# Two graph layers on one core: node preparation in four pieces, early masks and node tables on GpSimd, the first two rounds written out

## The chip, the core and the metric

The kernel runs on one NeuronCore of a Trainium2 chip. Five engines work beside each other, each through its own instructions in order: TensorE (PE) multiplies matrices, VectorE (DVE) and ScalarE (ACT) work element by element, GpSimd (POOL) does the same with general processors and also issues transfers, and SyncE (SP) issues most transfers. Engines wait for each other with semaphores. SBUF is the working memory of 128 partitions; PSUM is where PE writes its results, and POOL can't reach it.

The metric is the device time of one execution in microseconds (us). Smaller is better.

## The reference

There are N = 3327 nodes with D = 64 features and a 0/1 matrix `adj` (N by N). Two layers follow each other; each normalizes its input, takes the positive part `h`, and adds its result to `x`.

```python
# layer 0, on h = relu(layernorm(x))
x_t = logmap0(x, c)
left, right = x_t @ w_att[:D, 0], x_t @ w_att[D:, 0]
adj_att = sigmoid(left[:, None] + right[None, :] + b_att[0]) * adj
x_local = logmap(x[:, None, :], x[None, :, :], c)         # every pair of nodes
support_t = einsum('ij,ijd->id', adj_att, x_local)
return proj(expmap(x, support_t, c), c)
# layer 1, on h = relu(layernorm(x))
mask = (adj != 0); rank = cumsum(mask, axis=1); deg = rank[:, -1:]
k = minimum(deg, 100); pos = rank - (deg - k)
w = mask * where(pos > 0, 0.5 ** (k - pos), 0.0)          # the last neighbours of a row weigh most
return w @ (h @ weight) + bias
```

Layer 0 needs, for every pair of nodes, a sigmoid, the product of the two nodes' features and a function of it. Layer 1 needs, for every place of `adj`, the number of neighbours behind it in its row.

## The kernel before, in words

The nodes are padded to 26 blocks of 128. The function `fast` does all the work (`general` is a branch for inputs outside a range; it isn't entered here). The rows of the result are cut into four strips of 8, 8, 6 and 4 blocks. In each strip, a round takes one column block of `adj`, from the last to the first (two in the strip of 4), so that a round holds 128 x 1024 elements or 128 x 768. There are 91 rounds. One round does this, each step a function of its own:

- `load` (L613 to L618) brings the round's piece of the transposed `adj` into a tile `ad`, 512 KB, issued by SP; five tiles are in use in turn.
- `edges` (L620 to L623) makes the mask `ad != 0` in bf16, on DVE.
- `count` (L625 to L636) adds it, on PE, to a running number of neighbours in PSUM (`pc`), with two triangular constant matrices `ca` and `cb`.
- `read` (L638 to L649) takes the positive part out of `pc` into a small integer tile kept for layer 1. In strip 0 every second one is ACT's (`ON_ACT`), the others are DVE's.
- `sigmoids` (L651 to L656): ACT, a tanh of `left` (spread along the strip, `left_b`) with `right` as the bias.
- `products` (L668 to L674): PE, four matmuls into a tile `pq` in PSUM, of which there are two, from the features as columns (`ju`, `jz`) and as rows (`iu`, `iz`).
- two Gelu activations on `pq` in place (ACT, L1211 and L1212, in strip 0's first round L879 and L880).
- `pair_one` (L661) and `pair_two` (L666): DVE, sigmoid plus one times `ad`, and then times the function in `pq`.
- `total` (L676 to L684): PE, the sum over the round with the node table `hw` (65 columns, float32) into `po`.

After a strip, `post` finishes its nodes, with many small instructions on POOL, and after the last strip a second stage does layer 1's product (L1255 on).

Order: a manual schedule keeps PE, DVE and ACT in the order in which the code asks for work. POOL's and SP's instructions are placed by a scheduler, so the order of their lines in the code isn't the order in which they run. The loop at L1194 works n rounds at a time in a pipeline: while it multiplies round n, it makes the mask of n + 2, counts and reads n + 1, and prepares the sigmoids and products of n + 1.

Before the loop stands the preparation, which the change is about:

- x comes in two halves of 13 blocks, one issued by SP and one by ACT (L455, L456). For each half DVE takes the mean (L715) and the difference (L716), and ACT three activations (L717 to L719); then DVE reduces four times (L721, L722).
- A chain of small DVE instructions of 26 to 52 elements follows (L749 to L781 and L811 to L825): a Newton iteration for the inverse roots and constants of each node. Each mostly needs the one before it.
- `features` (L784) scales the features of the blocks that are needed first (strip 0's own blocks 0 to 7 and column blocks 24, 25); PE turns them (L831 to L838); copies bring them to `iu`, `ju`, `iz`, `jz` (L839 to L842). POOL's transfers (L846) copy them once more into `ju` and `jz` for the rounds that use blocks 0 to 7 as columns.
- The same follows for the column blocks 16 to 23 (`high`) and later 8 to 15 (`low`): `features`, casts, `turned_to` (L792), `kept` (L796, L797), and `logits` (L862 to L866) for `left` and `right`.
- Round 0 and the beginning of round 1 are written out between these (L869 to L899). The loop starts with round 1; in its first three passes it does `last_of_ahead`: the turning of `low`, the table `hw` in two parts (L907 to L915), the row of `left` sent to DRAM and back (L596 to L598), and eleven small constants of the nodes (L917 to L927).

Of the kernel before, what the change touches and what calls it, by code (L numbers as in the profile page):

```python
# [11 lines left out]
F32 = mybir.dt.float32  # L12
# [10 lines left out]
P = 128  # L23
N = 3327
NB = 26
# [7 lines left out]
AHEAD, LOADS = 1, 4  # L33
SGB, ADB = 5, 5
# [411 lines left out]
def fast(ctx, tc, x, adj_t, r, w_att, b_att, weight, bias, out, flag):  # L446
# [8 lines left out]
    nc.sync.dma_start(x_sb[:, :13], xv[:, :13])  # L455
    nc.scalar.dma_start(x_sb[:, 13:], xv[:, 13:])  # L456
# [137 lines left out]
    def left_to_dram():  # L594
        plt = ps.tile([P, P], F32, name="po")
        T.transpose(plt[:NB, :], left, ident)  # L596
        V.tensor_copy(left_t, plt[:NB, :])
        nc.sync.dma_start(left_d.rearrange("(b p) -> b p", p=P), left_t)  # L598
# [21 lines left out]
    def edges(n):  # L620
        mask_of[n] = mask = work.tile([P, FMAX], BF16, name="mask", bufs=3)
        args = mask[:, : span(n)], ad_of[n][:, : span(n)]
        V.tensor_scalar(*args, 0.0, None, op0=ALU.not_equal)  # L623
# [14 lines left out]
    def read(n, j):  # L638
        k, lo, hi = rounds[n]
        S = strips[k]  # L640
        kept = behind(j)[:, S.i0 : S.i0 + S.F]
        num, den = ON_ACT[k]
        i = NB - 1 - j
        if i * num // den != (i + 1) * num // den:
            A.activation(kept, S.pc[:, : S.F], AF.Relu, scale=128.0 if j in JD else 1.0)  # L645
        elif j in JD:
            V.tensor_scalar(kept, S.pc[:, : S.F], 0.0, 128.0, op0=ALU.max, op1=ALU.mult)
        else:
            V.tensor_scalar(kept, S.pc[:, : S.F], 0.0, None, op0=ALU.max)  # L649
# [63 lines left out]
    for hs in node_halves:  # L713
        n = hs.stop - hs.start
        V.tensor_reduce(m[:, hs], x_sb[:, hs], AX.X, ALU.add)  # L715
        V.scalar_tensor_tensor(d[:, hs], wide(m[:, hs], n), -1.0 / D, x_sb[:, hs], op0=ALU.mult, op1=ALU.add)  # L716
        A.activation(sq[:, hs], d[:, hs], AF.Square)  # L717
        A.activation(rl[:, hs], d[:, hs], AF.Relu)
        A.activation(sr[:, hs], rl[:, hs], AF.Square)  # L719
# [47 lines left out]
    G.memset(ju[D : KB + 7, first_i], -WB * QS)  # L767

# [29 lines left out]

    A.activation(g, g2, AF.Ln, bias=one_c, scale=-0.5)
# [26 lines left out]
    edges(0)  # L826
# [20 lines left out]

    V.tensor_mul(yr, yr, g[:, :NB])
# [6 lines left out]
    def logits(bs):  # L855

        plr = ps.tile([P, NB, 2], F32, name="po")
# [10 lines left out]
    for j in js(0):  # L868
        count(0, j)  # L869
    logits((first_i, last_j))  # L870
    V.tensor_sub(nz[:, high, 1], zf[:, high], nz[:, high, 0])
    for j in js(0):
        read(0, j)
# [3 lines left out]
    edges(1)  # L877
    pq = pq_of[0]
    A.activation(pq, pq, AF.Gelu, scale=-WG / QS)  # L879
    A.activation(pq, pq, AF.Gelu, scale=WH)  # L880
# [4 lines left out]
    for j in js(1):  # L885
        count(1, j)
    products(1)
    edges(2)
# [3 lines left out]
    for j in js(1):  # L892
        read(1, j)
    pair_two(0)
    logits((high,))
    features(low)
    A.copy(nz[:, low, 0], zf[:, low])
    V.tensor_copy(nu[:, low, :D], zf[:, low])
    V.tensor_sub(nz[:, low, 1], zf[:, low], nz[:, low, 0])  # L899

    def last_of_ahead():

        p4 = ps.tile([P, 16, P], F16, name="po")
        turned_to(p4, low, 0)
        kept(p4, low, 0)
        wn, opx = small("wn"), small("opx")
        V.tensor_scalar(wn, nrm, WA / 2, None, op0=ALU.mult)  # L907
        V.tensor_scalar(opx, x2, c_c, 1.0, op0=ALU.mult, op1=ALU.add)
        V.tensor_mul(hw[:, :, D], opx, wn)
        V.tensor_mul(wn, wn, y)  # L910
        V.tensor_mul(hw[:, 13:, :D], rl[:, 13:], wide(wn[:, 13:], 13))
        logits((low,))
        left_to_dram()
        yield
        V.tensor_mul(hw[:, :13, :D], rl[:, :13], wide(wn[:, :13], 13))  # L915
        yield
        V.tensor_scalar(w2s, w2, 2.0**27 / HS, None, op0=ALU.mult)  # L917
        V.tensor_scalar(ih, babs, 2 / WA, None, op0=ALU.mult)
        V.tensor_scalar(balm, bal, MIN_NORM, None, op0=ALU.max)
        V.tensor_mul(su, nrm, balm)  # L920
        V.tensor_mul(sv, bal, su)
        V.reciprocal(sk, balm)
        V.tensor_scalar(sk, sk, sqc, None, op0=ALU.mult)
        V.tensor_scalar(maxnorm, absr, 1.0 - EPS_BALL, None, op0=ALU.mult)
        V.tensor_mul(c2_c, c_c, c_c)
        V.tensor_scalar(m2c, c_c, -2.0, None, op0=ALU.mult)
        V.tensor_scalar(p2c, c_c, 2.0, None, op0=ALU.mult)  # L927
        ahead.close()

        behind_of["lo"] = ctx.enter_context(tc.tile_pool(name="lo", bufs=1, side="right", reuse_waits="tile")).tile(  # L930
            [P, JD.start, NP], U8, name="behind_lo")
        yield
# [261 lines left out]
    for n in range(1, R):  # L1194
# [7 lines left out]
        two = m < R and len(js(m)) == 2  # L1202
# [7 lines left out]
        pq = pq_of[n][:, :w]  # L1210
        A.activation(pq, pq, AF.Gelu, scale=-WG / QS)  # L1211
        A.activation(pq, pq, AF.Gelu, scale=WH)  # L1212
# [5 lines left out]
        if m + 1 < R:  # L1218
            edges(m + 1)
        if two:  # L1220
            read(m, js(m)[0])
        if m < R:
            count(m, js(m)[-1])
        if n + 1 < R:
            sigmoids(n + 1)
        if m < R:
            read(m, js(m)[-1])
        if n + 1 < R:
            products(n + 1)
        if n > 1 and not turned and not early:  # L1230
            total(n - 2)
# [148 lines left out]
```

## Time and profile before

| | |
|---|---|
| median of three executions | 418.3 us (418.13, 418.3, 419.4) |
| profiled execution, whole time | 419.95 us |
| its span in the profile | 418.2 us |
| mean granted TensorE clock | 0.973 |
| busy: PE, DVE, ACT, POOL | 359.9, 377.5, 362.8, 113.4 us |
| bytes moved | 48.99 MB, mean 117 GB/s |
| largest groups on DVE | L666 103.5 us, L661 103.8 us, L623 58.7 us |
| largest group on PE | L683 162.2 us |

The profile is one execution. Its span runs from the first to the last instruction that it saw; the whole time is somewhat longer. An engine's busy time is the time in which it executed; issuing transfers and waiting for semaphores are not in it. A row of a view in order of time gives the start, the duration, the engine with the line, the operation, the tile written and the tiles read, the shapes, and in brackets the engine's idle time before the instruction and what ended it. Instructions on DVE and ACT overlap a little, so that the time from one start to the next can be some 0.08 us less than the duration.

### The profile page before, as it was taken

The numbers are of one execution on the slowest core, as the hardware profiler recorded it, in microseconds if no ns is written. First come the engines' busy times: TensorE is split into PE (matmuls) and PEld (weight loads), VectorE is DVE, ScalarE is ACT, GpSimd is POOL, SyncE is SP. The second block draws the span as 40 slices with busy tenths as digits, with TensorE's granted clock in tenths as the row PEclk, the third lists the DMA queues.
The fourth block names the chain that finished last, engine by engine and source line by source line (L and its number), as shares of the span: only waits on it lengthen the run. The fifth ranks groups of instructions, "written<-read, shape, count | busy, mean of one in ns | idle before, by whom it ended". The sixth has DMA issues, their size and how long they took to land. (4 is left out here: it accounts for less than half of the span.)

```text
span 418.2 us, 4717 instructions
## 1 busy us (share of the span) xinstructions
PE 359.9 (86%) x1460; PEld 154.2 (37%) x1460; DVE 377.5 (90%) x559; ACT 362.8 (87%) x409; POOL 113.4 (27%) x224
## 2 busy tenths in 40 slices
PE   0094999999998899999999899999877999898792
PEld 0062333333333333333333444444332333344362
DVE  4989999999999999999999998899989899898841
ACT  3577889999999999999999999999896999787810
POOL 7020000000000073950250063801405183442400
PEclk9999799999999999999999999999898999999987
DMA  7313634444547445444535455444633420000012
GB/s 180 160 40 102 191 100 153 150 153 150 155 146 233 138 127 175 141 121 143 147 116 159 113 152 146 123 146 127 186 116 103 113 88 0 2 0 1 2 25 65
DMA packets 23298, 48.99 MB, mean 117 GB/s; under 512 B 8789, under 2 KB 9245, under 8 KB 23265
## 3 DMA queue, kind: packets, MB, share of 16 engines
q1 hardware_dynamic: 20993, 47.66, 37.9%
q0 software_dynamic: 464, 0.49, 0.7%
q10 hardware_dynamic: 1808, 0.46, 0.6%
q8 instruction: 13, 0.21, 0.2%
q14 instruction: 20, 0.16, 0.1%
HBM read 46.40 MB, written 0.87 MB: 113 GB/s over the span
## 5 line engine op out<-in xcount | busy, mean ns | idle before, releaser
L683 PE MATMUL po<-sg,hw 128*65 128x512 f32 (+1 forms) x364 | 162.2, 570 | 0.4 <-DVE st L958 0.4
L666 DVE SCALAR_TENSOR_TENSOR sg<-pq,sg 128x1024 f32<-128x1024 f32 (+1 forms) x91 | 103.5, 1137 | 7.4 <-ACT pq L1212 6.8
L661 DVE SCALAR_TENSOR_TENSOR sg<-sg,ad 128x1024 f32<-128x1024 f32 (+1 forms) x91 | 103.8, 1140 | 0.1
L656 ACT ACTIVATE sg<-left_b,right 128x1024 f32<-128x1024 f32 (+2 forms) x103 | 99.5, 978 | 0.0
L1211 ACT ACTIVATE pq<-pq 128x1024 f32<-128x1024 f32 (+1 forms) x90 | 86.1, 957 | 2.7 <-PE pq L674 2.5
L1212 ACT ACTIVATE pq<-pq 128x1024 f32<-128x1024 f32 (+1 forms) x90 | 85.2, 946 | 2.9
L683 PEld LDWEIGHTS po<-sg,hw 128*65 128x65 f32 x364 | 49.7, 139 | 70.8 <-issue 56.9
L634 PE MATMUL pc<-mask,ca 128*128 128x512 bf16 (+1 forms) x175 | 64.3, 368 | 12.4 <-DVE behind_hi L649 3.8
L673 PE MATMUL pq<-iu,ju 71*128 71x512 f16 (+1 forms) x182 | 67.8, 373 | 1.5 <-ACT jz L797 1.0
L635 PE MATMUL pc<-mask,cb 128*128 128x512 bf16 (+1 forms) x182 | 65.5, 370 | 1.8 <-ACT behind_lo L645 1.7
L674 PE MATMUL pq<-iz,jz 128*128 128x512 f16 (+1 forms) x182 | 66.3, 371 | 0.0
L623 DVE TENSOR_SCALAR mask<-ad 128x1024 bf16<-128x1024 f32 (+1 forms) x91 | 58.7, 645 | 0.0
L1280 PE MATMUL pw<-wt,s 128*128 128x512 bf16 (+1 forms) x154 | 34.2, 376 | 4.2 <-DVE s L1135 2.2
L635 PEld LDWEIGHTS <-cb 128*128 128x128 bf16 x182 | 17.9, 98 | 53.2 <-issue 41.5
L1030 POOL TENSOR_TENSOR dots<-dots,ih 128x8 f32<-128x8 f32 (+1 forms) x3 | 2.2, 720 | 129.0 <-DVE dots L1050 129.0
L634 PEld LDWEIGHTS <-ca 128*128 128x128 bf16 x175 | 17.3, 99 | 29.6 <-issue 17.7
L1280 PEld LDWEIGHTS <-s 128*128 128x128 f16 x182 | 18.0, 101 | 23.8 <-issue 4.3
L673 PEld LDWEIGHTS <-ju 71*128 71x128 f16 x182 | 18.0, 99 | 22.8 <-DVE sg L666 4.3
L674 PEld LDWEIGHTS <-jz 128*128 128x128 f16 x182 | 18.1, 100 | 19.5 <-issue 2.3
L645 ACT ACTIVATE behind_lo<-pc 128x1024 uint8<-128x1024 f32 (+2 forms) x29 | 24.9, 858 | 0.0
L645 ACT ACTIVATE behind_hi<-pc 128x1024 uint8<-128x1024 f32 (+2 forms) x23 | 19.7, 858 | 5.6 <-PE pc L635 5.6
L1285 POOL TENSOR_TENSOR x_sb<-x_sb,bias_b 128x256 f32<-128x256 f32 (+1 forms) x6 | 9.9, 1657 | 51.0 <-DVE w L1119 45.5
(317 smaller groups left out, 366.8 us busy)
## 6 DMA issues: line engine op xcount, KB each, us to landing
ad<-in_adj_t SPq DMA_DIRECT2D x65, 512.0 KB, 3.6
ad<-in_adj_t SPq DMA_DIRECT2D x26, 384.0 KB, 3.2
out<-o SPq DMA_DIRECT2D x6, 128.0 KB, 1.9
left_b<-left_d SPq DMA_DIRECT2D x1, 512.0 KB, 4.0
x_sb<-in_x ACTq DMA_DIRECT2D x1, 416.0 KB, 5.6
x_sb<-in_x SPq DMA_DIRECT2D x1, 416.0 KB
left_b<-left_d SPq DMA_DIRECT2D x1, 384.0 KB
jz<-iz POOLq DMA_DIRECT2D x2, 128.0 KB, 2.6
```

The source lines that it names most:

```text
L623: V.tensor_scalar(*args, 0.0, None, op0=ALU.not_equal)
L634: T.matmul(S.pc[:, f0:f1], ca, S.before[:, f0:f1], start=False, stop=True, skip_group_check=True)
L635: T.matmul(S.pc[:, f0:f1], cb, now[:, f0:f1], start=S.first, stop=True, skip_group_check=True)
L656: A.activation(part(n, sg, j), S.left[:, : S.F], AF.Tanh, bias=right[:, j : j + 1], scale=0.5)
L661: V.scalar_tensor_tensor(sg, sg, 1.0, ad_of.pop(n)[:, :w], op0=ALU.add, op1=ALU.mult)
L666: V.scalar_tensor_tensor(sg, pq_of.pop(n)[:, :w], WD, sg, op0=ALU.add, op1=ALU.mult)
L673: T.matmul(part(n, pq, j, f0, f1), ju[:KB, j, :], S.iu[:, f0:f1], start=True, stop=False)
L674: T.matmul(part(n, pq, j, f0, f1), jz[:, j, :], S.iz[:, f0:f1], start=False, stop=True)
L683: T.matmul(S.po[: D + 1, f0:f1], hw[:, j, :], part(n, sg_of[n], j, f0, f1), start=j == NB - 1, stop=j == 0)
L1211: A.activation(pq, pq, AF.Gelu, scale=-WG / QS)
L1212: A.activation(pq, pq, AF.Gelu, scale=WH)
L1280: T.matmul(pw[n], s2[:, j].rearrange("p c d -> p (c d)"), wt[:, f0:f1].bitcast(BF16), start=j == order[0], stop=j == NB - 1)
```

## The change

- x comes in four pieces of 7, 6, 7 and 6 blocks, issued by SP and ACT in turn, and the first loop on it runs over these pieces. The four reductions stay on halves.
- `edges` takes an engine. The masks of rounds 0 to 2 (`EARLY`) are made on POOL, which compares with zero twice (`is_equal`, `is_equal`); those of later rounds stay on DVE.
- `read` takes an order to use ACT. Rounds 0 to 2 use it. `count` and `read` of round 0 move to the place before the logarithms of the preparation.
- The table `hw` is made on POOL, in seven pieces of up to 4 blocks, the last blocks first. Nine of the eleven node constants move to POOL; `balm` and its reciprocal stay on DVE.
- The features of `low` are made between rounds 0 and 1, turned into a `pq` tile (not `po`), and the logits of `low` and the row of `left` use the same tile.
- Rounds 0 and 1 are written out whole; the loop starts with round 2, and two pieces of `adj` more than four are loaded ahead of it.

In the program as built, POOL runs after its first constants the masks of rounds 0, 1 and 2, then five small constants, then `opx`, `ih`, `wn`, the seven pieces of `hw`, and only then the transfers of the turned features. On PE `count` of round 0 stands ahead of the transposes, and `count` of round 1 right behind them, ahead of the first logits.

```diff
+EARLY = 3
...
-    nc.sync.dma_start(x_sb[:, :13], xv[:, :13])
-    nc.scalar.dma_start(x_sb[:, 13:], xv[:, 13:])
+    pieces = (slice(0, 7), slice(7, 13), slice(13, 20), slice(20, NB))
+    for n, part in enumerate(pieces):
+        (nc.scalar if n % 2 else nc.sync).dma_start(x_sb[:, part], xv[:, part])
...
-    def edges(n):
+    def edges(n, E=V):
         mask_of[n] = mask = work.tile([P, FMAX], BF16, name="mask", bufs=3)
         args = mask[:, : span(n)], ad_of[n][:, : span(n)]
-        V.tensor_scalar(*args, 0.0, None, op0=ALU.not_equal)
+        if E is G:
+            G.tensor_scalar(*args, 0.0, 0.0, op0=ALU.is_equal, op1=ALU.is_equal)
+        else:
+            V.tensor_scalar(*args, 0.0, None, op0=ALU.not_equal)
...
-    def read(n, j):
+    def read(n, j, on_act=None):
...
-        if i * num // den != (i + 1) * num // den:
+        if on_act or (on_act is None and i * num // den != (i + 1) * num // den):
...
-    for hs in node_halves:
+    for hs in pieces:
...
     G.memset(ju[D : KB + 7, first_i], -WB * QS)
+    for n in range(EARLY):
+        edges(n, G)
...
+    for j in js(0):
+        count(0, j)
+        read(0, j, True)
     A.activation(g, g2, AF.Ln, bias=one_c, scale=-0.5)
...
-    edges(0)
...
+    wn, opx = small("wn"), small("opx")
+    G.tensor_scalar(wn, nrm, WA / 2, None, op0=ALU.mult)
+    G.tensor_scalar(opx, x2, c_c, 1.0, op0=ALU.mult, op1=ALU.add)
+    G.tensor_mul(hw[:, :, D], opx, wn)
+    G.tensor_mul(wn, wn, y)
+    for b in (24, 20, 16, 12, 8, 4, 0):
+        n = min(4, NB - b)
+        G.tensor_mul(hw[:, b : b + n, :D], rl[:, b : b + n], wide(wn[:, b : b + n], n))
...
-    for j in js(0):
-        count(0, j)
+    for j in js(1):
+        count(1, j)
     logits((first_i, last_j))
     V.tensor_sub(nz[:, high, 1], zf[:, high], nz[:, high, 0])
-    for j in js(0):
-        read(0, j)
+    for j in js(1):
+        read(1, j, True)
     products(0)
     pl = first_left()
     turned_to(p3, high, 0)
-    edges(1)
...
+    gelus(0)
     strips[0].left, left_b = pl, strips[0].left
     sigmoids(0)
     kept(p3, high, 0)
     pair_one(0)
-    for j in js(1):
-        count(1, j)
+    features(low)
+    V.tensor_copy(nu[:, low, :D], zf[:, low])
     products(1)
-    edges(2)
...
     sigmoids(1)
-    for j in js(1):
-        read(1, j)
+    A.copy(nz[:, low, 0], zf[:, low])
     pair_two(0)
     logits((high,))
...
+    for j in js(2):
+        count(2, j)
+    pair_one(1)
     V.tensor_sub(nz[:, low, 1], zf[:, low], nz[:, low, 0])
+    gelus(1)
+    p5 = ps.tile([P, FMAX], F32, name="pq", bufs=2)
+    p4 = p5.bitcast(F16).rearrange("p (b q) -> p b q", q=P)
+    turned_to(p4, low, 0)
+    total(0)
+    sigmoids(2)
+    edges(3)
+    kept(p4, low, 0)
+    for j in js(2):
+        read(2, j, True)
+    pair_two(1)
+    products(2)
+    logits((low,), p5[:, : 2 * NB].rearrange("p (b c) -> p b c", c=2))
+    left_to_dram(p5[:, FMAX - P :])
...
     def last_of_ahead():
-        p4 = ps.tile([P, 16, P], F16, name="po")
-        turned_to(p4, low, 0)
-        kept(p4, low, 0)
...
-        V.tensor_mul(hw[:, 13:, :D], rl[:, 13:], wide(wn[:, 13:], 13))
-        logits((low,))
-        left_to_dram()
+        V.tensor_scalar(balm, bal, MIN_NORM, None, op0=ALU.max)
+        V.reciprocal(sk, balm)
         yield
-        V.tensor_mul(hw[:, :13, :D], rl[:, :13], wide(wn[:, :13], 13))
-        yield
-        V.tensor_scalar(w2s, w2, 2.0**27 / HS, None, op0=ALU.mult)
+        G.tensor_scalar(w2s, w2, 2.0**27 / HS, None, op0=ALU.mult)
...
     load(LOADS)
-    for n in range(1, R):
+    load(LOADS + 1)
+    for n in range(2, R):
```

## The prediction

> **What bounds the kernel now.** I read the table of busy times, then the busy times in stretches, then DVE's and POOL's rows in order of time up to 60 us, and last the few rows where POOL and DVE work side by side.
>
> ```profile
> span 418.2 us, 4717 instructions
> PE 359.9 (86%) x1460; PEld 154.2 (37%) x1460; DVE 377.5 (90%) x559; ACT 362.8 (87%) x409; POOL 113.4 (27%) x224
> ...
> 34.00:44.00 10.00, 4.44 (x44) 2.66 (x44) 9.28 (x19) 7.59 (x10) 0.00 (x0) 0.82 0.37 116
> 44.00:54.00 10.00, 10.00 (x29) 3.61 (x28) 9.37 (x20) 8.04 (x8) 0.19 (x1) 0.84 0.54 175
> 54.00:64.00 10.00, 10.00 (x36) 3.83 (x35) 9.93 (x15) 8.86 (x9) 0.00 (x0) 1.00 0.39 115
> 64.00:94.00 30.00, 30.00 (x107) 11.49 (x106) 29.93 (x35) 29.71 (x32) 0.00 (x0) 1.00 0.50 155
> ```
>
> In the stretches the columns after the width are PE, PEld, DVE, ACT and POOL, then granted clock. From 64 to 94 us PE, DVE and ACT are all full: a round there takes what its instructions take, and the change touches none of them. It can only bring the steady rounds forward or put them back. Before 54 us one engine is near full, DVE, while PE idles (4.44 of 10 us) with its clock at 0.82 and 0.84.
>
> My mark is DVE's second multiply of a round (L666), which ends the round's work on DVE:
>
> ```profile
> 5.96 1.02 DVE L715 TENSOR_REDUCE m<-x_sb 128x13 f32<-128x832 f32 x1 [5.96 <-DMA x_sb<-in_x]
> 14.15 0.17 DVE L749 TENSOR_SCALAR v<-v 128x26 f32<-128x26 f32 x1
> 23.54 0.69 DVE L839 COPY iu<-pq 71x1024 f16<-71x1024 f16 x1
> 32.60 1.21 DVE L666 SCALAR_TENSOR_TENSOR sg<-pq,sg 128x1024 f32<-128x1024 f32 x1
> 39.02 1.21 DVE L666 SCALAR_TENSOR_TENSOR sg<-pq,sg 128x1024 f32<-128x1024 f32 x1
> 45.29 1.21 DVE L666 SCALAR_TENSOR_TENSOR sg<-pq,sg 128x1024 f32<-128x1024 f32 x1
> 50.83 1.21 DVE L666 SCALAR_TENSOR_TENSOR sg<-pq,sg 128x1024 f32<-128x1024 f32 x1
> 55.15 1.22 DVE L666 SCALAR_TENSOR_TENSOR sg<-pq,sg 128x1024 f32<-128x1024 f32 x1
> ```
>
> Start, duration, instruction: the wait for x, the start of the chain of small node instructions, the first copy of turned features, and the marks of rounds 0 to 4. Steps: 9.06 us from the copy to round 0, then 6.42, 6.27, 5.54 and 4.32. I work out when the mark of round 4 comes after the change; what it gains is what the kernel gains.
>
> **Can POOL work for nothing beside DVE?** That decides this change, so these rows first:
>
> ```profile
> 291.21 2.53 POOL L1285 TENSOR_TENSOR x_sb<-x_sb,bias_b 128x256 f32<-128x256 f32 x2 [18.52 <-DVE w L1119]
> 293.26 1.31 DVE L661 SCALAR_TENSOR_TENSOR sg<-sg,ad 128x768 f32<-128x768 f32 x1
> ...
> L661 DVE SCALAR_TENSOR_TENSOR sg<-sg,ad 128x768 f32<-128x768 f32 x26 | 25.0, 961 | 0.0
> ...
> L1285 POOL TENSOR_TENSOR x_sb<-x_sb,bias_b x6: 715/1978/2313, 205.1 to 388.1; 128x256 f32<-128x256 f32 x5, 128x384 f32<-128x384 f32 x1
> ```
>
> Two POOL adds end at 293.74. DVE's multiply that starts inside the second takes 1.31 us, not its usual 0.95: it lost 0.36 us and went on 0.12 us before POOL was done. The same adds take 0.715 us at best and about 2 us in the middle: against DVE instructions that follow each other closely POOL waits. So whichever has started holds the other up. In the steady rounds DVE leaves no opening. In the node chain it does, about 0.1 us after each instruction (the next needs its result). I therefore let each POOL instruction that reads hold DVE for its duration less 0.12 us while DVE is in that chain. Nothing (DVE undisturbed) and the whole duration are the ends.
>
> The Trainium skill speaks against the change here: "SBUF — State Buffer", section "Who interferes with whom", has DVE and GpSimd share a port pair, locked for the whole instruction, against DVE instructions with two SBUF inputs or in a two-port mode; reductions and reads of PSUM are exempt. The row above is its case; that the small instructions of the chain are caught too, no run here shows.
>
> **The change part by part.**
>
> x in quarters. The first half of x released DVE at 5.96; its packets run from about 1.9 us. A first piece of 7 of 13 blocks comes at 1.9 + 4.04 x 7/13 = 4.1 (the transfer view from 1 to 3 us has 874 packets on that queue and the piece has 896, so not before 3.0; if the pieces land together, 5.96). The later pieces land by about 6.2, the total being the same. DVE's pairs cost 1.2 and 1.1 us (448 and 384 elements at 1.0 us per 832, and 0.1 each), so they end near 8.7; four reductions of 0.93 us follow, held up a little by ACT's six added instructions (0.1 us each, by the casts of 512 and 128 elements, 0.51 and 0.20 us apart). L749 comes at 12.55 instead of 14.15: **-1.6** (ends 0 and -2).
>
> Masks. GpSimd's compare is not in the trace. Nearest is the cast of 128 elements, 0.34 us, beside 0.19 for a copy of 8: 1.25 ns an element, so 1.5 us for 1024. Ends: 1.0 us (memset of 128, 0.27 against 0.17 for 8) and 2.3 us (the add, 0.715 for 256). The skill's "GPSIMD Engine Reference", section "Engine selection", calls one input roughly line rate; at its 1.2 GHz that is an estimate of 0.85 + 0.19 = 1.04 us, which would make the sum 0.9 us better. Mask 0 runs from 9 to 11 us beside DVE's reductions and costs nothing; ACT's added reading of round 0 fills ACT's idle time before 19 us. Taking mask 0 from DVE gives nothing at once either, since L839 then waits for PE's transposes (PE ends them at 23.5). Masks 1 and 2 have to wait for their blocks, which land about 11.4 and 12.1 us after issue, at 13 and 14.2, in the middle of DVE's node chain: 2 x 1.38, and some 0.4 for the small constants put between: **+3.15** (0 to +5).
>
> Summing table hw. In POOL's order its seven multiplies stand ahead of the transfers of L846; those serve column blocks needed only 18 rounds on. They start once wn is there, near 21 us, and hold the pair 6 x 0.6 + 0.35 = 3.95 us beside the second half of DVE's node chain (L811 to L825). About 1.2 of it falls into openings, and 0.75 takes the place of the wait for PE just named: **+2.0** (0 to +4). The copy iu comes at 23.54 - 1.6 + 3.15 + 2.0 = 27.1, that is 3.55 late.
>
> Now the written-out rounds, on DVE, in times to the next start (L666, L661, L649 1.13; a mask 0.6; copy of turned features 0.6):
> - copy to round 0, 9.06: off a reading and two masks (2.33), on the low features and their cast (1.05). The rest is a chain through PE's transposes and ACT's sigmoid, and the waits there grow by 0.9: -0.4.
> - 0 to 1, 6.42: off features and cast (1.4) and a reading (1.13), on the copy of the low features (0.6) and a short wait: -1.8.
> - 1 to 2, 6.27: off the table's first half (1.8) and the copy (0.6), on a wait of some 1.4 more for the low logits, which stand on PE behind ACT's copy of jz: -1.0. p4 and the left row in a products' tile leave the sums' tile free, so round 0's sums run in this step too, in PE's idle time (4.44 us busy of 10); without that cover their 1.9 us (four rows of L683 in steady rounds) would stand ahead of round 2's products.
> - 2 to 3, 5.54: off the table's second half (0.94) and a wait for PE (0.52), on balm and its reciprocal (0.45): -1.0.
> - 3 to 4, 4.32: off the eleven node constants (1.46): -1.45.
>
> Together -5.65, and with +3.55 the mark of round 4 comes **2.1 us** earlier. ACT takes over two readings (1.0 us each), mostly in idle time (2.4 us before 40.9, 4.3 before 19). PE's waits of 4 us before 42 us go, and with them perhaps the half clock; DVE is the later one there, so no further gain. If the clock falls again, PE pays some 1.5 us: 0.82 and 0.84 over two stretches of 10 us come to 3.4, and about half of that was on the path.
>
> Profiled time before: 419.95 us (span 418.2 and 1.75 around it), 1.65 over the median of 418.3. 419.95 - 2.1 = 417.85; on the median, **416.2 us**.
>
> **Rivals.** 0.3% (1.25 us) is about what can be told from no change.
> - DVE is hardly held up (its requests go first, or POOL is near 1 us a mask). Without the +5.15 the copy comes at 21.9; then more of the rounds hang on PE and ACT (the chain to round 0 then takes 10.2, not 8.65), so 3.6 of it remains: 2.1 + 3.6 = 5.7 faster, **412.6**. For it: DVE's steady rows hardly ever show a delay. Against it: the 1.31 us row. Chance 0.22.
> - GpSimd's work holds DVE longer than its best rows say: slower. Place: masks 1 and 2 and the multiplies in the node chain. At 2.3 us a mask (+1.6) and 1.2 us a multiply (+3.4; their middle row is 1.98) the mark comes 2.9 late: **421.2**. From 2.1 us more holding in all the change loses. Against it: 1.98 includes POOL's own waiting. Chance 0.18.
> - It doesn't do what it says at the front: the quarters land together (+1.6), or PE's clock halves again around 40 us (+1.5): **417.8**, hardly to be told from no change. Chance 0.17.
> - The forecast, gains of 0.9 to 3.5: 0.43.
>
> **How the numbers follow.** Faster by over 0.3%: the first rival, 0.36 of the forecast and 0.04 of the third: 0.62. Within: 0.07 + 0.11 + 0.03 of the slower rival: 0.21. Slower: 0.15 and 0.02: 0.17. The range, 412 to 420, takes in the first rival's time and half of the second's; it leaves out about 1 in 10 on each side.
>
> **What would show it.** L715's first row near 4.1 and L749's near 12.5; POOL masks of 1.5 us at 9, 13 and 14.5 with openings or long rows on DVE beside them (right), or DVE's node rows at their usual spacing (first rival); copy iu near 27, marks near 35.7, 40.4, 45.6, 50.1 and 53.0; PE's granted clock at 1.00 from 34 to 54. Wrong if the steady rounds after 60 us change their 3.45 us, or if POOL's later transfers hold up a strip.

## The result, and the profile after

In 20 executions of each, taken in turn on one chip, the median is **421.86 us** (416.2 to 424.52) after the change and 419.45 us (417.6 to 421.43) before it. The ratio is 0.9999 with a 95% interval of 0.9976 to 1.0023, and 1.0062 (1.0034 to 1.0089) in a second set of executions of the same two kernels (the first experiment below); it leaves out executions more than 1.5% above the fastest of their kernel, which are eight of the 20 of the kernel after in the first set and none in the second. So the change doesn't make the kernel faster; by the medians it costs 2.4 us in the first set and 2.3 in the second. The forecast was 416.2 us.

What has to be explained is double: the median is 5.7 us over the forecast, and the executions lie over 8.3 us, where those of before lie over 3.8. (Of the 5.7 us, 1.15 is the kernel before, whose median here is 419.45 and not the 418.3 that the forecast started from.)

The profiled execution of the kernel after happens to be one of its quicker ones: 418.39 us. Its page begins:

```profile
span 416.4 us, 4722 instructions
...
PE 357.0 (86%) x1437; PEld 152.5 (37%) x1460; DVE 374.6 (90%) x543; ACT 365.4 (88%) x417; POOL 134.0 (32%) x247
```

POOL has 20.6 us more work, DVE 2.9 us less. The busy times in the stretches shown of before (same columns) are:

```profile
34.00:44.00 10.00, 8.19 (x66) 4.44 (x67) 8.10 (x16) 9.11 (x11) 0.00 (x0) 0.83 0.48 137
44.00:54.00 10.00, 9.95 (x35) 3.71 (x34) 9.96 (x13) 9.94 (x11) 2.24 (x4) 1.00 0.59 179
54.00:64.00 10.00, 9.90 (x36) 3.81 (x35) 9.90 (x17) 9.90 (x11) 0.00 (x0) 1.00 0.44 149
64.00:94.00 30.00, 29.53 (x101) 10.89 (x102) 29.97 (x33) 29.45 (x31) 0.00 (x0) 1.00 0.52 157
```

The steady rounds are what they were, and the idle time of PE from 34 to 44 us is mostly gone, as worked out. Its granted clock is still 0.83 there, where 1.00 was forecast, and 1.00 from 44 us on. The same steps on DVE (the multiply is L670 now, the chain's start L753, the copy L847):

```profile
4.36 0.62 DVE L719 TENSOR_REDUCE m<-x_sb 128x7 f32<-128x448 f32 x1 [4.36 <-DMA x_sb<-in_x]
...
10.02 0.55 DVE L719 TENSOR_REDUCE m<-x_sb 128x6 f32<-128x384 f32 x1 [1.34 <-DMA x_sb<-in_x]
...
15.69 0.17 DVE L753 TENSOR_SCALAR v<-v 128x26 f32<-128x26 f32 x1
...
26.41 0.69 DVE L847 COPY iu<-pq 71x1024 f16<-71x1024 f16 x1 [0.64 <-PE pq L846]
...
35.80 1.22 DVE L670 SCALAR_TENSOR_TENSOR sg<-pq,sg 128x1024 f32<-128x1024 f32 x1
...
40.48 1.21 DVE L670 SCALAR_TENSOR_TENSOR sg<-pq,sg 128x1024 f32<-128x1024 f32 x1
...
45.81 1.20 DVE L670 SCALAR_TENSOR_TENSOR sg<-pq,sg 128x1024 f32<-128x1024 f32 x1
...
50.23 1.21 DVE L670 SCALAR_TENSOR_TENSOR sg<-pq,sg 128x1024 f32<-128x1024 f32 x1
...
53.10 1.21 DVE L670 SCALAR_TENSOR_TENSOR sg<-pq,sg 128x1024 f32<-128x1024 f32 x1
```

The five marks are within 0.25 us of the forecast (35.7, 40.4, 45.6, 50.1, 53.0), and yet the start of the node chain (L753) is off by 3.1 us: the fourth piece of x is reduced at 10.02, after 1.34 us of waiting for its transfer, and the chain starts at 15.69 instead of the predicted 12.55. Errors that cancel, that is luck, made this execution look right. The late piece of x is the first suspect for the others.

Three masks take POOL 10.92 us instead of 4.5. The view in order of time of POOL has them in one row, that of DVE the instructions they hold up:

```profile
10.60 10.92 POOL L625 TENSOR_SCALAR mask<-ad 128x1024 bf16<-128x1024 f32 x3 [1.47 <-DMA ad<-in_adj_t]
```

```profile
10.61 1.46 DVE L720 SCALAR_TENSOR_TENSOR d<-m,x_sb 128x384 f32<-128x384 f32 x1
...
17.95 0.99 DVE L747 TENSOR_TENSOR w_h<-w_lr,w_h 128x2 f16<-128x2 f32 x1
...
20.76 0.79 DVE L784 TENSOR_SCALAR s<-s,sqc 128x26 f32<-128x26 f32 x1
20.88 0.68 DVE L785 SCALAR_TENSOR_TENSOR yz<-nrm,zs_c,y 128x26 f32<-128x26 f32 x1
```

These four take 0.56, 0.15, 0.14 and 0.25 us when nothing is beside them. In the 10.92 us DVE lost 2.8 us of row time, in rows near the beginnings and ends of the masks; the four reductions and some 30 small instructions between ran at their usual pace.

### The profile page after: what moved, and what is told of

Its sections match the earlier page's. It is cut to its first block, busy times and chain, and to the rows that moved or that the text cites. A ratio compares the mean times of both kernels' runs of the same rounds, so it can differ in the third digit from the quotient of the medians.

```text
span 416.4 us, 4722 instructions
## 1 busy us (share of the span) xinstructions
PE 357.0 (86%) x1437; PEld 152.5 (37%) x1460; DVE 374.6 (90%) x543; ACT 365.4 (88%) x417; POOL 134.0 (32%) x247
## 4 chain that ended last, share of the span: by engine, by line
DVE 41%; ACT 28%; PE 13%; issue 12%; POOL 3%; DMA 2%; ACTq 0%; DVEq 0%; POOLq 0%
DVE sg L670 12%; DVE sg L665 10%; ACT sg L660 9%; ACT pq L873 8%; PE po L687 4%; ACT pq L874 3%; DVE wt L1286 3%; DVE behind_lo L653 3%; ACT behind_hi L649 2%; DMA x_sb<-in_x 2%; ACT behind_lo L649 2%; DVE behind_hi L653 2%; PE pw L1298 2%; PE pw L1327 1%; PE pq L677 1%
## 5 line engine op out<-in xcount | busy, mean ns | idle before, releaser
L670 DVE SCALAR_TENSOR_TENSOR sg<-pq,sg 128x1024 f32<-128x1024 f32 (+1 forms) x91 | 103.6, 1138 | 7.0 <-ACT pq L874 6.4
L874 ACT ACTIVATE pq<-pq 128x1024 f32<-128x1024 f32 (+1 forms) x91 | 86.2, 947 | 2.9
L873 ACT ACTIVATE pq<-pq 128x1024 f32<-128x1024 f32 (+1 forms) x91 | 87.1, 958 | 1.6 <-PE pq L678 1.1
L639 PE MATMUL pc<-mask,cb 128*128 128x512 bf16 (+1 forms) x169 | 61.3, 372 | 16.6 <-POOL mask L625 14.3
L638 PE MATMUL pc<-mask,ca 128*128 128x512 bf16 (+1 forms) x169 | 62.3, 368 | 11.5 <-DVE behind_hi L653 3.9
L677 PE MATMUL pq<-iu,ju 71*128 71x512 f16 (+1 forms) x182 | 66.8, 367 | 3.3 <-ACT jz L803 2.0
L627 DVE TENSOR_SCALAR mask<-ad 128x1024 bf16<-128x1024 f32 (+1 forms) x88 | 56.8, 646 | 0.0
L1298 PEld LDWEIGHTS <-s 128*128 128x128 f16 x182 | 18.0, 100 | 23.6 <-issue 4.2
L649 ACT ACTIVATE behind_hi<-pc 128x1024 uint8<-128x1024 f32 (+2 forms) x25 | 21.8, 871 | 4.4 <-PE pc L639 3.6
```

The source lines that it names most:

```text
L638: T.matmul(S.pc[:, f0:f1], ca, S.before[:, f0:f1], start=False, stop=True, skip_group_check=True)
L639: T.matmul(S.pc[:, f0:f1], cb, now[:, f0:f1], start=S.first, stop=True, skip_group_check=True)
L670: V.scalar_tensor_tensor(sg, pq_of.pop(n)[:, :w], WD, sg, op0=ALU.add, op1=ALU.mult)
L677: T.matmul(part(n, pq, j, f0, f1), ju[:KB, j, :], S.iu[:, f0:f1], start=True, stop=False)
L1298: T.matmul(pw[n], s2[:, j].rearrange("p c d -> p (c d)"), wt[:, f0:f1].bitcast(BF16), start=j == order[0], stop=j == NB - 1)
```

## The experiments

Twelve kernels, each against the kernel before on the same chip. All compute the whole result. "Last x" is the start of the last first-reduction (L719 of after), "chain" that of the node chain (L753), "s to g" the stretch from the last clamp of `s` (L787) to the last logarithm step (L834), marks are DVE's second multiply of rounds 0 and 4; these columns come from one profiled execution, the median from all.

| kernel | last x | chain | s to g | mark 0 | mark 4 | profiled | median (range, executions) | ratio to before |
|---|---|---|---|---|---|---|---|---|
| before | 7.96 | 14.15 | 3.71 | 32.60 | 55.15 | 419.95 | 419.45 (417.6 to 421.4, 20) | |
| after | 10.02 | 15.69 | 3.72 | 35.80 | 53.10 | 418.39 | 421.86 (416.2 to 424.5, 20) | 0.9999 (0.9976 to 1.0023) |
| e1 after, again | 13.24 | 18.01 | 6.05 | 39.08 | 56.38 | 421.14 | 421.71 (418.5 to 424.5, 12) | 1.0062 (1.0034 to 1.0089) |
| e2 one queue for x | 10.16 | 14.94 | 3.72 | 37.33 | 56.10 | 420.74 | 421.26 (419.5 to 425.5, 12) | 1.0075 (1.0044 to 1.0106) |
| e3 x in halves | 8.05 | 14.63 | 3.73 | 35.89 | 53.31 | 419.82 | 418.71 (417.2 to 420.9, 12) | 0.9989 (0.9967 to 1.0010) |
| e4 masks on DVE | 14.07 | 18.84 | 6.04 | 40.86 | 58.16 | 421.73 | 421.26 (418.4 to 426.1, 12) | 1.0028 (1.0007 to 1.0049) |
| e5 before, x in quarters | 13.64 | 18.41 | 3.70 | 36.56 | 58.95 | 423.48 | 422.73 (417.3 to 424.2, 12) | 1.0030 (0.9997 to 1.0062) |
| e6 adj held back | 8.59 | 13.38 | 4.26 | 35.19 | 52.49 | 417.12 | 417.39 (416.5 to 419.7, 9) | 0.9961 (0.9939 to 0.9982) |
| e7 weights late | 13.02 | 17.79 | 5.19 | 39.27 | 56.58 | 421.29 | 422.80 (421.1 to 426.3, 8) | 1.0090 (1.0061 to 1.0118) |
| e8 halves, free places | 8.00 | 14.20 | 4.07 | 34.61 | 51.91 | 420.74 | 417.51 (416.0 to 421.3, 12) | 0.9959 (0.9929 to 0.9988) |
| e9 table late | 8.99 | 13.76 | 4.18 | 36.14 | 53.44 | 420.80 | 423.32 (418.6 to 425.4, 10) | 1.0056 (1.0022 to 1.0089) |
| e10 e8, quarters, adj held | 7.49 | 12.29 | 4.08 | 31.81 | 49.21 | 416.85 | 416.83 (414.4 to 420.3, 12) | 0.9928 (0.9893 to 0.9963) |
| e11 e8, PE kept busy | 7.89 | 14.08 | 4.25 | 33.88 | 52.52 | 417.70 | 417.81 (416.9 to 419.5, 12) | 0.9959 (0.9937 to 0.9981) |
| e12 both | 8.61 | 13.43 | 4.73 | 33.59 | 50.98 | 417.93 | 416.59 (416.2 to 417.9, 6) | 0.9917 (0.9890 to 0.9943) |

### The late quarter, or the masks

Theory X: the last quarter of x lands late, by an amount that differs between executions. Theory H: GpSimd's masks hold DVE by such an amount.

**e1** is the kernel after, unchanged.

> The changed kernel once more, to see how far its executions lie apart and what a second profile shows. Theory X (the last quarter of x lands late, by an amount that differs from one execution to the next, since it stands behind blocks of adj on the transfer engines, and this shifts everything behind it): times spread over 5 us or more, median 419 to 422 us; in the profile the last quarter's first reduction (L719) starts later than 8 us, and the mark of round 4 (L670) moves with it. Theory H (POOL's masks hold DVE in the node chain by an amount that differs): the same times, but a slower profile than the first has longer DVE rows between L753 and L834, and L719 starts where it did.

Another execution in the profile, 2.75 us longer. Its rows on DVE:

```profile
13.24 0.55 DVE L719 TENSOR_REDUCE m<-x_sb 128x6 f32<-128x384 f32 x1 [4.56 <-DMA x_sb<-in_x]
...
18.01 0.17 DVE L753 TENSOR_SCALAR v<-v 128x26 f32<-128x26 f32 x1
...
30.44 0.68 DVE L847 COPY iu<-pq 71x1024 f16<-71x1024 f16 x1
```

The last quarter is reduced 3.22 us later than in the first profile, the mark of round 4 comes 3.28 us later, and the whole execution takes 2.75 us more. The masks ran at the same times as there (from 10.78, 3.6 us each).

**e2** issues all four pieces on SP's queue.

```diff
-        (nc.scalar if n % 2 else nc.sync).dma_start(x_sb[:, part], xv[:, part])
+        nc.sync.dma_start(x_sb[:, part], xv[:, part])
```

> The changed kernel with all four quarters of x on SP's queue, ahead of the blocks of adj in the same queue. Theory X: nothing can overtake the last quarter; it is there by about 6.5 us, L753 starts near 13 us and not 15.7, the mark of round 4 near 50.5 to 52 us, the median falls to 415.5 to 418 us, and the times lie within 4 us of each other. Theory H: the order of x's pieces matters little, the median stays at 419 to 422 us and the times still lie 6 to 8 us apart.

No cure: the fourth piece is still late (10.16), though it stands ahead of adj in the same queue, and the masks, which begin at 12.2 here, hold the chain up by 3.6 us (8.40 from the chain's start to the last clamp of `s`, 4.79 before). **e3** takes x in halves and keeps everything else.

```diff
-    pieces = (slice(0, 7), slice(7, 13), slice(13, 20), slice(20, NB))
+    pieces = node_halves
```

> The changed kernel with x in two halves again, in its transfers and in the first loop; all else stays. Theory X: the halves land at about 6 and 6.5 us as in the kernel before, L753 starts near 14.2 us, the mark of round 4 near 52 us, the median is 416 to 418.5 us and the times lie within 4 us. Theory H: no better than the changed kernel, 419 to 422 us, spread 6 to 8 us.

The median falls by 3.0 us and the range from 6.0 to 3.7 us, that of the kernel before. **e4** keeps the quarters and makes the three masks on DVE, behind Newton's steps.

```diff
-        edges(n, G)
+        edges(n)
```

> The changed kernel with the masks of rounds 0 to 2 on DVE again, at the place in DVE's order behind the Newton steps. Theory X: DVE pays 3 x 0.6 us and gets back 1.3 us of holding, so the median stays within 1.5 us of the changed kernel and the spread stays at 6 to 8 us. Theory H: the median falls by 2 to 4 us to 416 to 418.5 us and the times lie within 4 us.

The spread stays (7.7 us, of which the two longest executions make 4.4), and the last quarter comes at 14.07. So the masks aren't the cause of the spread; X holds. The granted clock differs between executions too (last section), but it isn't the cause either: at one mean clock, 0.976 to 0.977, the five executions of e3 lie within 1.0 us (417.20 to 418.15), and those of the kernel after over at least 5.0 (416.95 to 421.95).

### What the quarter stands behind

**e5** is the kernel before with nothing but the four pieces (its two issues and its first loop as in the diff of the change).

> The kernel before with nothing but x in quarters (masks, summing table and rounds as they were). Theory X (the split into quarters is what makes the last quarter of x late, by an amount that differs from execution to execution): the last first-reduction starts at 10 to 14 us of the span instead of 7.96, the node chain (the first step after the reductions) starts at 15.7 to 18.8 instead of 14.15, the second multiply of round 4 is as much later (56.7 to 60), the median is 421 to 424 us against some 419.4, and the executions lie over 6 us or more. Rival theory (quarters are harmless by themselves; the spread comes from GpSimd's masks, which begin when the blocks of adj land): last first-reduction by 8 us, chain at 12.6 to 14.2, median 417.5 to 419.5, spread not over 4 us.

```profile
13.64 0.55 DVE L716 TENSOR_REDUCE m<-x_sb 128x6 f32<-128x384 f32 x1 [4.98 <-DMA x_sb<-in_x]
...
18.41 0.17 DVE L750 TENSOR_SCALAR v<-v 128x26 f32<-128x26 f32 x1
```

The quarters alone cost the kernel before 2.85 us in the median, and spread its executions from 3.6 to 7.0 us. The ratio's interval just reaches 1, so the profile's rows and the spread say more here than the ratio. **e6** is the kernel after, with the first loads of adj held until the fourth quarter is reduced. **e7** is the kernel after, with bias and weight, which GpSimd transfers at the start, issued behind the masks.

```diff
+        if held:
+            V.memset(ad[:, :1], 0.0)
         nc.sync.dma_start(ad[:, : span(n)]...
...
     for hs in pieces:
...
+    for n in range(LOADS):
+        load(n, True)
```

```diff
     for n in range(EARLY):
         edges(n, G)
+    bias_b = across(bias, D, "bias_b")
+    for half in (slice(0, D), slice(D, P)):
+        nc.gpsimd.dma_start(w2[half], weight)
```

> The kernel after, with the first four loads of adj held on SP's queue until the fourth quarter of x has been reduced (VectorE clears one column of each adj tile behind that quarter, and the load waits for it; nothing is left out). Theory A (x's last packets stand behind adj's 4 KB packets): the last first-reduction starts by 7.5 us instead of 10.0 to 14.1, the node chain by 13.5; adj lands from about 11 us on, so that the three masks on GpSimd end at 23 to 25; round 4's second multiply at 51 to 54, median 416 to 419, spread at most 5 us. Theory P (they stand behind the transfers of GpSimd's queue, 2 KB packets of about 1.1 us each): the last first-reduction stays at 10 us or later, adj and the masks come 4 us or more later than that, and the median is 423 or more.

> The kernel after, with the transfers of bias (the 2 KB packets) and weight issued by GpSimd behind the three masks instead of at the start; nothing is left out. Theory P (x's last packets stand behind GpSimd's transfers): the last first-reduction starts by 7.5 us, the node chain by 13.5, median 417 to 419.5 with a spread of at most 5 us. Theory A (they stand behind adj's blocks): the last first-reduction stays at 10 to 14 us in the profile, median 420 to 422.5, spread 6 us or more.

The transfer issues of the first 12 us, in the kernel after and in e6 (queue, KB each, microseconds from issue to landing):

```profile
ad<-in_adj_t SPq DMA_DIRECT2D x5, 512.0 KB, 10.7
x_sb<-in_x SPq DMA_DIRECT2D x2, 224.0 KB, 3.5
x_sb<-in_x ACTq DMA_DIRECT2D x2, 192.0 KB, 6.3
```

```profile
ad<-in_adj_t SPq DMA_DIRECT2D x5, 512.0 KB, 6.0
x_sb<-in_x SPq DMA_DIRECT2D x2, 224.0 KB, 3.4
x_sb<-in_x ACTq DMA_DIRECT2D x2, 192.0 KB, 5.3
```

and e6's rows on DVE, then e7's:

```profile
8.59 0.55 DVE L719 TENSOR_REDUCE m<-x_sb 128x6 f32<-128x384 f32 x1
...
13.38 0.17 DVE L755 TENSOR_SCALAR v<-v 128x26 f32<-128x26 f32 x1
```

```profile
13.02 0.55 DVE L716 TENSOR_REDUCE m<-x_sb 128x6 f32<-128x384 f32 x1 [4.79 <-DMA x_sb<-in_x]
```

With adj out of the way the last reduction no longer waits for a transfer (8.59, no bracket; I had expected 7.5), the range shrinks to 3.2 us and the median to 417.39. Moving GpSimd's transfers doesn't help (422.8). So it is adj's loads, whose 4 KB packets begin on SP's queue 5.3 us into the span, that make the fourth quarter late: theory A. The traces' packets say the same. Where adj is not held, the last packet of x on ACT's queue ends at 8.6 to 13.4 us (six kernels with quarters on two queues); where it is held, at 7.66 (e6), 5.75 (e10) and 5.84 (e12), before adj's first packet, which begins at 9.65 or later. The holding also lets adj's blocks land 6.0 us after issue instead of 10.7, so that it costs the masks only 3 us of start.

The Trainium skill's "DMA: Bandwidth & Descriptors", section "Queues, rings and completion order", says that each transfer engine takes a packet from each queue that has work in turn. The rows agree only in part: a packet of x takes 18 ns, one of adj 159 ns, and the last 92 packets of x on ACT's queue took from 7.0 to 12.65 us in e1. But 289 packets of x were left there when adj began at 5.3 us; one of each in turn on 16 transfer engines would take 289 / 16 x 177 ns = 3.2 us (an estimate from these rows), and they took 7.4. With halves some 190 packets of x were left when adj began, and they were through 0.5 us later. And in e2 x stands ahead of adj in one queue and was still through only at 9.80 us; from 5 to 7 us that queue kept 28% of the transfer engines busy. So that adj's loads do it is shown for two queues; how they do it, and what holds the one queue up in e2, no run here settled.

### The rest of the change with x undisturbed

**e8** has x in halves and puts the other parts where they lie beside nothing: mask 0 on DVE behind Newton's steps, mask 1 behind `g`, mask 2 behind the high features (where DVE waited 1.28 us), the table's first product on DVE behind the first logits, so that POOL's multiplies come after the chain.

```diff
-    for n in range(EARLY):
-        edges(n, G)
+    edges(0)
...
+    edges(1)
     iz, iu = strip_in(0)
...
     V.tensor_sub(nz[:, high, 1], zf[:, high], nz[:, high, 0])
+    edges(2)
+    V.tensor_scalar(wn, nrm, WA / 2, None, op0=ALU.mult)
+    ... (the table's lines on POOL follow here)
```

> The rounds written out as in the kernel after, but x in halves, the masks of rounds 0 to 2 on VectorE (mask 0 behind Newton's steps, mask 1 where VectorE waits for the transposes, mask 2 where it waits for the high features' transposes), and the summing table on GpSimd only behind the first logits, so that nothing of GpSimd's runs beside the node chain. If the lost gain went to the late quarter, to the masks' holds (1.3 us) and to the table beside the chain, all three are gone: chain at 14.2, second multiply of round 0 at 32.5 to 33.5, of round 4 at 50 to 51.5 (55.15 in the kernel before, 53.10 after), median 414.5 to 416 against 419.4, spread at most 4 us. If instead the time is set behind round 4 whatever comes before it, 418 to 419.5.

Faster than before, by 0.4% (0.12 to 0.71). But the stretch from `s` to `g` is 0.36 us longer (DVE waits 0.53 us for ACT, which has just read round 0), and round 0's mark comes 10.25 us after the copy, not 8.65: the marks miss what I expected by 0.4 to 1.1 us, the median by 1.5. **e9** is the kernel after with only the table put behind the first logits.

> The kernel after with one edit: the first product of the summing table (26 columns) is made by VectorE behind the first logits, so that GpSimd's seven multiplies of the table can't begin before; x stays in quarters, the masks stay on GpSimd. Theory T (the table's multiplies lie beside the node chain whenever x is late, and hold VectorE there): even with a last first-reduction at 13 us or later, the stretch from the clamps of s to g is 3.7 to 4.2 us as in the kernel before, not 6.0, and the median comes to 419.5 to 420.8 instead of 421.7, the spread to 5 us or less. Rival (the 6.0 us have another reason, the chain is slow because adj's loads or the masks run beside it): the stretch stays at 5.5 to 6 us, median 421 to 422.5.

Inconclusive: in the profiled execution the last quarter came early (8.99), so that its 4.18 us don't test the theory; the median, 423.32, lies above what either expected. The pair e4 and e5 tells more. Both have their masks on DVE and a chain that starts at 18.4 to 18.8; with the table on POOL the stretch from `s` to `g` takes 6.04 us, without it 3.70. In e1, the table's row on POOL and four of the rows on DVE beside it:

```profile
25.51 4.46 POOL L863 TENSOR_TENSOR hw<-rl,wn 128x128 f32<-128x128 f32 x7
```

```profile
26.04 0.64 DVE L825 TENSOR_TENSOR nu<-as__229,nu 128x26 f16<-128x26 f32 x1
...
27.15 1.10 DVE L828 TENSOR_TENSOR nzi<-sq,nzi 128x512 f16<-128x512 f32 x1
28.17 0.64 DVE L829 COPY nu<-nu 128x78 f16<-128x78 f16 x1
...
28.80 0.70 DVE L831 TENSOR_TENSOR d<-sq,d 128x128 f16<-128x128 f32 x1
```

They took 0.27, 0.69, 0.23 and 0.27 us in the first profile, where the table came later than them. So a late chain costs once more: 2.3 us here, of which 0.75 comes back in round 0, where the table then is out of the way.

**e10** is e8 with quarters and adj held (the edits of the change and of e6). **e11** is e8 with 30 transposes on PE that nothing uses, before the first count. **e12** is both.

```diff
+    warm = ps.tile([P, P], F32, name="po")
+    for _ in range(30):
+        T.transpose(warm, sr[:, 24:26].rearrange("p c d -> p (c d)"), ident)
     for j in js(0):
         count(0, j)
```

> The version with halves, masks on VectorE and a late table, given quarters of x again, with adj's first four loads held behind the fourth quarter. If the quarters' own gain is real once adj is out of the way: node chain at 13.2 to 13.5 instead of 14.2, round 4's second multiply at 50.8 to 51.2 instead of 51.9, median about 0.8 us below that version's 417.5, so 416.2 to 417. If holding adj costs as much as the quarters give (a mask that waits for its block): 417.3 to 418.5.

> The version with halves, masks on VectorE and a late table, with 30 more TensorE transposes of 128x128 (their output is used by nothing) from about 13 us on, ahead of the first count. Theory W (that version's first round is 1.6 us longer than worked out because TensorE, which had been idle, runs its 512-column matmuls in 0.63 us instead of 0.38 until 30.6 us): the matmuls from 21.7 us on take 0.38, the stretch from the copy of iu to round 0's second multiply falls from 10.25 to 8.0 to 8.8, round 4's second multiply from 51.9 to 50 to 50.5, median 415.3 to 416.3 against 417.5. Rival (the rate is the throttle's and has nothing to do with what TensorE did before): 0.63 us as long as now, stretch 10 to 10.5, median 417 to 418.

> Both additions together: quarters with adj held, and the 30 transposes. If both act and add up: node chain at 13.2 to 13.5, round 0's second multiply at 31.3 to 32.3, round 4's at 48.8 to 49.7, median 414.3 to 415.5, which would be 4 to 5 us under the kernel before. If neither acts: 417 to 418.

e10's rows:

```profile
12.29 0.17 DVE L755 TENSOR_SCALAR v<-v 128x26 f32<-128x26 f32 x1
...
22.45 0.69 DVE L850 COPY iu<-pq 71x1024 f16<-71x1024 f16 x1
...
31.81 1.21 DVE L672 SCALAR_TENSOR_TENSOR sg<-pq,sg 128x1024 f32<-128x1024 f32 x1
...
49.21 1.21 DVE L672 SCALAR_TENSOR_TENSOR sg<-pq,sg 128x1024 f32<-128x1024 f32 x1
```

Quarters do gain once nothing stands before them: the chain starts at 12.29, the mark of round 4 comes 5.9 us earlier than before and 2.7 earlier than in e8. The median is 0.7 us below e8's, which the intervals of the two ratios can't tell from nothing. In e11 PE's matmuls of 512 columns do run in full from 23.6 us on, as one and the same line shows in e8 and then in e11 (512 columns, in order of time):

```profile
26.78 0.63 PE L678 MATMUL pq<-iz,jz 128*128 128x512 f16 x1
```

```profile
25.87 0.38 PE L678 MATMUL pq<-iz,jz 128*128 128x512 f16 x1
```

but the copy to round 0 takes 9.52 us, not 8.0 to 8.8, and a window of half clock at 37.6 us then makes the step from round 1 to 2 6.47 us instead of 5.34. The time doesn't fall (417.81). So the slow matmuls are real and follow from PE's idle time, and are only some 0.7 of the 1.6 us missed in e8. e12 has the smallest ratio, 0.9917, from six executions; its difference from e10 is smaller than either interval.

## Why the prediction was wrong

Its steps, against the profiled execution of the kernel after and against e1, which is the more typical one. The last column is e6, where adj is held. All are differences to the kernel before, in us.

| step | predicted | after | e1 | e6 |
|---|---|---|---|---|
| chain's start, "x in quarters" | -1.6 | +1.54 | +3.86 | -0.77 |
| chain to the last clamp of `s`, "masks" | +3.15 | +1.32 | +1.42 | +2.95 |
| `s` to the copy iu, "summing table" | +2.0 | +0.01 | +1.62 | +0.83 |
| copy to round 0 | -0.4 | +0.33 | -0.42 | -0.42 |
| 0 to 1, 1 to 2, 2 to 3, 3 to 4 | -1.8, -1.0, -1.0, -1.45 | -1.74, -0.94, -1.12, -1.45 | -1.73, -0.94, -1.12, -1.46 | -1.74, -0.93, -1.12, -1.46 |
| sum at round 4 | -2.1 | -2.05 | +1.23 | -2.66 |

- **The step that failed** is "The later pieces land by about 6.2, the total being the same". It took the packets' mean rate for all there is. The last piece lands at about 9, 10, 13 or 14 us, because adj's loads start before it is through (e6, e10, e12), and differently in each execution. Against the forecast the chain starts 3.1 us late in the execution profiled first, of which 0.9 is the fourth piece's L720 beside a mask, and 5.5 in e1, where that row takes its usual 0.56. With adj held the term is right or nearly so: the chain starts at 12.29 in e10 against 12.55 worked out, and at 13.4 in e6 and e12. The prediction had no term for what makes this difference: in e6 and e12 the second piece's L720 takes 1.44 and 1.54 us beside POOL's first constants, in e10 0.56. The rival that named the quarters had them land together, at 5.96; that they could land after what the halves did was not among the cases.
- **The masks** were mis-sized. One takes 3.64 us (10.92 / 3), not 1.5, beyond the upper end of 2.3. But POOL's instruction doesn't hold DVE for its whole length: in the first profile the chain lost 1.3 us and L720, ahead of it, 0.9, together 2.2 against 3.15. What the masks cost the chain isn't one value either. From its start to the last clamp of `s` it was 1.3 to 1.4 us in the kernel after, e1 and e3, and 2.2 to 3.6 in e7, e9, e6 and e2, so that the forecast 3.15 lies inside what was measured, by two errors that go against each other: masks more than twice as long, and a hold of less than their length. The cited rule, a lock for the whole instruction, would have stopped DVE's two-input instructions for all of the 3.6 us of each mask; the rows above show delays of 0.4 to 0.9 us. The estimate of 1.04 us a mask, from the skill's line rate, is less than a third of the 3.64 measured.
- **The table** came at 25.8 us instead of 21, since the masks took POOL until 21.5 and its small instructions until 25.7. In the first profile that is behind the chain, and round 0 comes some 0.7 us later than worked out; with a late chain it lies beside it (e1, e4).
- **The written-out rounds** were right: the five steps sum to -4.92 and -5.67 against -5.65. With x and POOL undisturbed they show in the time (e8, e10).
- "What it gains is what the kernel gains": from the mark of round 4 to the end of DVE's last instruction these executions take the same time (355.88 us after the change, 355.84 before, 355.87 in e1), so here the mark was a fair measure. What wasn't fair was to expect one value for it. In e8 and e10 it isn't even fair: the same stretch takes 360.0 and 358.6 us, with three and two more windows of half clock in it (last section).
- The slower rival's 421.2 us is near the measured median by luck. It had masks of 2.3 us and the table's multiplies hold DVE, and the mark come 2.9 us late. In e1, where the mark comes 1.2 late, masks and table cost 3.0 us, less than the forecast's 5.15; what put the mark behind the forecast is the 5.5 us at the chain's start.

The direction "faster" is what e6 shows: with the quarter no longer late, the change gives 417.39 us, its ratio is 0.39% below 1 (0.18 to 0.61), not far from the forecast of 0.5%, and the mark of round 4 comes 2.66 us earlier against 2.1 forecast. The steps behind this sum agree less well than the sum.

## What to carry to other kernels

Splitting a load let the first piece come sooner, but here its last piece came late beside the loads that followed; look at the landing of the last piece in several executions, and hold the next big loads back until it is in. A profile that agrees with a forecast in one execution proves little where the executions are spread: compare the steps one by one, and the profile's own time with the median. Work given to an idle engine wasn't free here where it lay beside DVE's chain: the order of POOL's own work (masks, then table) decided which part of DVE's chain it met.

## What the runs showed of the hardware that I had not expected

- GpSimd's two-comparison pass over 128x1024 float32 into bf16 takes 3.62 to 3.67 us in the seven kernels that have it, some 3.5 ns an element in each partition; DVE's one-comparison pass takes 0.69.
- PE's matmuls of 512 columns take 0.63 us up to 27.5 us of the span in the kernel after and 0.38 from 28.4 us on; 30 transposes ahead of them bring them to 0.38 at 23.6 us (e11). The views print a granted clock of 1.00 for the slow stretch, but the first clock record of the trace stands at 28.28 us (31.13 in e8, 17.08 in e11), so the printed 1.00 tells nothing of the time before.
- The granted clock falls to half for windows of 3.4 us, and their number differs between executions of one kernel, which spreads the times also where x is in time. Of e8's twelve, five at a mean clock of 0.976 to 0.977 took 415.99 to 417.91 us (four of them under 416.3), and four at 0.965 to 0.966 took 420.74 to 421.31. The Trainium skill's "TensorE: Matmul & The Clock Gate", section "What's actually happening", has the clock judged in windows of 3.4 us that run on freely, whatever the program does. The traces agree: in all fourteen of them the clock's records begin and end on a grid of 3.41 us. The stretches show two strips' ends in e10 and then the same two in the kernel after, each window with the one behind it (width, then PE's busy time first and granted clock third from the end):

```profile
129.10:132.50 3.40, 1.09 (x11) 0.84 (x12) 3.06 (x5) 2.07 (x4) 0.00 (x0) 1.00 0.51 154
132.50:135.90 3.40, 3.40 (x9) 1.31 (x7) 3.40 (x5) 3.40 (x5) 0.00 (x0) 0.50 0.35 81
...
224.70:228.10 3.40, 1.91 (x18) 1.13 (x16) 2.85 (x6) 3.31 (x6) 0.00 (x0) 1.00 0.48 150
228.10:231.50 3.40, 3.40 (x10) 1.46 (x8) 3.40 (x6) 3.40 (x6) 0.00 (x0) 0.50 0.37 110
```

```profile
130.68:134.09 3.41, 2.06 (x8) 0.69 (x7) 3.41 (x5) 2.68 (x3) 0.00 (x0) 1.00 0.64 187
134.09:137.50 3.41, 2.20 (x16) 1.23 (x16) 3.07 (x4) 2.80 (x5) 0.00 (x0) 1.00 0.25 100
...
226.25:229.66 3.41, 1.92 (x11) 0.80 (x9) 3.41 (x6) 3.35 (x6) 0.00 (x0) 1.00 0.54 137
229.66:233.07 3.41, 3.36 (x20) 1.93 (x22) 2.86 (x6) 3.38 (x6) 0.00 (x0) 1.00 0.37 104
```

PE pauses at these strips' ends. Where 1.09 or 1.91 of the 3.4 us were busy, the next window ran at half clock; where 2.06, 2.20 or 1.92 were, it didn't. Over all windows on this grid at full clock in the fourteen traces, half clock followed in 48 of 48 with PE busy for less than 1.6 us, in 23 of 94 with 1.6 to 2.4, and in none of 1361 with more; since 1.91 and 1.92 went different ways, PE's busy time as the profile has it isn't the whole rule. So how the pause falls on the grid decides with it whether a strip's end costs a window at half clock. Behind the mark of round 4, e8 has six such windows and e10 five, where the kernel after has three, and they take 4.1 and 2.8 us longer to DVE's last instruction: some 1.4 us a window. A kernel that comes earlier by 2 us can gain or lose that in single executions.
